# A norm's transposes move from the slot that projects values to the next slot, which projects outputs

## Chip, cores and metric

One Trainium2 chip, one of its cores. The metric is device microseconds (us) from the start to the end of one execution. The kernel before was run three times; the median is what the change is compared with. One further execution was recorded by the hardware profiler, and all durations of single instructions come from that one.

## What is computed

A transformer block in float32 for two sequences (B = 2) of 1024 rows with 256 features, and for each a context of 154 rows with 192 features. There are 16 heads of 64.

```python
h = layernorm(x, ln1);  x = attention(h, h, sa_wq, sa_wk, sa_wv, sa_wo) + sa_bo + x
h = layernorm(x, ln2);  x = attention(h, context, ca_wq, ca_wk, ca_wv, ca_wo) + ca_bo + x
h = layernorm(x, ln3);  p = h @ ff_w1 + ff_b1
out = (p[:, :1024] * gelu(p[:, 1024:])) @ ff_w2 + ff_b2 + x
# attention: softmax(q k^T / 8) v for each of 16 heads
```

## The kernel before

TensorE (PE) does all matmuls and transposes, VectorE (DVE) the maxima of the scores and the 32x32 block transposes of the weights, ScalarE (ACT) the exponentials and most copies out of PSUM, GpSimd (POOL) the scaling by the reciprocal sums and small arithmetic, and the queue of SyncE (SP) issues nearly all DMAs. Every engine works through its instructions in the order in which the program emits them (`manual_schedule`), so the Python order below is each engine's order.

**Self-attention** is a loop over 128 steps `p` (line 1062). A unit is one sequence and one pair of heads; there are 16 units (eight pairs of the first sequence, then eight of the second), and each has eight steps. Every step starts with `self_first`: two groups of scores (L488, 16 instructions each) into the two `ps_s` banks, and two maxima (L650). After that come, in this order: the stores left over from the step before (`flush(stores)`), the four exponentials (L499), the exchange of maxima and sums by four small DMAs (L509), POOL's joining of the step before (L517 to L525, with an ACT exponential at L521), two block transposes on DVE (L614), an addition to x if one is due (L469), and a reciprocal (L596) with four scalings on POOL (L600). The rest of the step is one of these, by p mod 8:

- 0 and 1: the next unit's queries, then keys (L357).
- 4, called the value slot here: the next unit's values (L388).
- 5, called the output slot: two pieces of the output projection (L462), and in some units an extra matmul group `context_ends` (L743).
- 2, 3, 6 and 7, called sum slots: half of a sum of values weighted by the transposed weights (L535) into two accumulators `po`. Slot 2 or 6 opens the two accumulators, 3 or 7 closes them; in the step after that ACT copies them out (L635).

What a slot's matmuls leave in PSUM is copied out by a "store" that is not emitted at once: it waits in the list `stores` until the next step's `flush(stores)`, which stands behind that step's scores and ahead of its exponentials.

**The norms beside it.** While these steps run, the norm that is needed next is done bit by bit. `norm_beside` puts steps k into the list `side`; `run_work` takes one of them in the value slot and one in the output slot of a unit, behind the value projection and ahead of the output pieces. Two norms are done so inside self-attention: the first norm of the second sequence (called at unit 1, so steps k = 0, 1, 2 ... fall on p = 12, 13, 20, 21, 28, 29 ...), and the second norm of the first sequence (called at unit 9, p = 76, 77, 84, 85 ...). For these two, which `narrow` tells from the other three, a step k handles one tile of 128 rows (n = 1); pairs of tiles are then worked on together:

- statistics (DVE, L235 and L236) at every k up to 7,
- the deviation of a pair (POOL, L241 and L245) at k = 2, 4, 6, 8, so always in a value slot,
- `normalize` of a pair (DVE L251, then two ACT instructions L265 into the tile `xn`, of which there is one buffer) at k = 3, 5, 7, 9, so always in an output slot,
- `turn` of a pair (four TensorE transposes L275 from `xn` into one PSUM bank `ph`; its store is four ACT instructions L290, which apply gain and shift and write `hT`) at k = 4, 6, 8, 10, so always in a value slot.

Within a step k the functions run in the order of the tuple in line 330: `turn` first, `normalize` last.

The PSUM bank for `ph` comes from the pool `ps_o`, because both slots call `run_work` with `sum_tile`. That pool has two banks in all, tag `po`. It also holds the two accumulators of the sum slots and the bank `pe` of `context_ends`:

```python
ps_o = ctx.enter_context(tc.tile_pool(name="ps_o", bufs=2, space=bass.MemoryType.PSUM))   # L67
run_work(2 if p < SA - SH else 1, h % 2 or h == 0, sum_tile)                               # L1086
halves[h, "po"] = [bank(f"po_{h}_{a2}") for a2 in range(2)]                                # L623
```

After the loop come 48 steps of cross-attention and then the feed-forward part, whose norms are not `narrow` and keep their steps.

Of the kernel before, what the change touches and what calls it, by code (L numbers as in the profile page):

```python
# [18 lines left out]
def tile_transformer_block(ctx: ExitStack, tc: tile.TileContext, a: dict, out: bass.AP):  # L19
# [12 lines left out]
    NT = S // P  # L32
# [64 lines left out]
    for n in names:  # L97
        k = n_of[n]
# [200 lines left out]
    def tile_order(kind):  # L299

        if kind == "ff":
            return list(range(NT))
        return [t for i in range(NT // 2) for t in (i, NT // 2 + i)]

    def narrow(kind, b):

        return kind == "sa" or kind == "ca" and b < B - 1

    def add_biases(kind, b):

        bo = {"sa": "sa_bo", "ca": "ca_bo", "ff": "ff_b2"}[kind]

        def add(t):
            xs = xt[b, t // GT][:, t % GT, :]
            nc.gpsimd.tensor_tensor(xs, xs, bias[bo], ALU.add)

        later.extend(lambda t=t: add(t) for t in range(NT))
        if b == B - 1 and kind != "ff":
            later.append(lambda: load_bias({"sa": "ca_bo", "ca": "ff_b2"}[kind]))

    def norm_beside(kind, b):

        after = {"sa": None, "ca": "sa", "ff": "ca"}[kind]
        stats, deviation, normalize, turn = norm_pieces(kind, b)
        n = 1 if narrow(kind, b) else 2
        lag = {}
        for fns, first in ((turn, 3), (stats, 0), (deviation, 1), (normalize, 2)):  # L330
            for i, fn in enumerate(fns):
                t = i if fns is stats else 2 * i + 1
                lag.setdefault(first + t // n, []).append((fn, fns is turn))
        for k in range(NT // n + 3):
            tiles = tile_order(kind)[k * n:(k + 1) * n]
            needs = [(after, b, half, t) for half in range(NQ) for t in tiles if after]

            def step(fns=lag[k]):
                done = [fn() for fn, _ in fns]
                return next((fn for fn in done if fn), None)  # L340

            side.append((any(turns for _, turns in lag[k]), needs, step))
        if not narrow(kind, b):
            side.append((False, (), lambda: add_biases(kind, b)))

# [198 lines left out]
    side, lates = [], []  # L544
# [118 lines left out]
    def self_beside(ui):  # L663

        nxt = self_pieces(*units[ui + 1]) if ui + 1 < NU else cross_pieces(*units[0])
        if ui + 1 < NU:
            work.extend(nxt)
        else:

            work.extend(nxt[:1])  # L670
            held.extend(nxt[1:])
        if ui >= HP:
            ob, og = divmod((ui - HP) // HP, NQ)
            t0 = (ui % HP) * 2
            out_pieces("sa", ob, og, out_order("sa")[t0:t0 + 2])
        if ui == 1:
            norm_beside("sa", 1)
        if ui in (4, 6):
            add_biases("sa", (ui - 4) // 2)
        if ui == NPAIR + 1:  # L680
            norm_beside("ca", 0)
# [214 lines left out]
    def cross_beside(ui):  # L896

        if ui == 2:
            norm_beside("ca", B - 1)
        if ui > HP + 1:  # L900
            ob, og = divmod((ui - HP - 2) // HP, NQ)
            t0 = ((ui - HP - 2) % HP) * 2
            out_pieces("ca", ob, og, out_order("ca")[t0:t0 + 2])
        if ui == NU - 5:
            norm_beside("ff", 0)
# [98 lines left out]
    with tc.manual_schedule():  # L1004
        stats, deviation, normalize, turn = norm_pieces("sa", 0, True)
# [56 lines left out]
        for p in range(SA):  # L1062
# [21 lines left out]
            if h == 0 or hg < LAG:  # L1084
# [4 lines left out]
                ui, n = divmod(p, 2 * SH)  # L1089
# [13 lines left out]
        for c in range(CA):  # L1103
# [13 lines left out]
            ui, n = divmod(c, len(CG))  # L1117
# [125 lines left out]
```

## Time and profile before

| | us |
|---|---|
| median of three runs | 1113.07 (1111.95 to 1114.58) |
| the profiled execution, whole | 1114.26 |
| its span, first to last instruction | 1112.5 |
| PE busy | 1092.5 |
| DVE, POOL, ACT busy | 855.3, 684.7, 626.1 |
| first scores of self-attention | at 17.63 |
| scores of its unit 15 (last) | at 673.2 |

A row of the timeline reads: start in us, duration in us of the merged instructions, engine, source line, operation, tile written <- tiles read, shape, number of instructions. Square brackets at the end give how long the engine stood idle just before and what ended that idle time. For matmuls the duration runs from the first start to a modelled end, so neighbours may overlap by some tenths of a microsecond. A row of the busy windows reads: stretch, its length, then busy time and number of instructions for PE, weight loads, DVE, ACT and POOL, the granted TensorE clock (1.00 is full), the share of DMA engines in use, and GB/s.

### The profile page before, as it was taken

Reading aid. Unit: us, or ns where it says so; the run is one execution under the profiler, and the core shown is the slowest. Engines: PE = TensorE matmul, PEld = TensorE weight load, DVE = VectorE, ACT = ScalarE, POOL = GpSimd, SP = SyncE. Lnnn points to the kernel's source line nnn. Section 1 sums busy time; section 2 is a strip of 40 time slices with the busy share of each in tenths; the row PEclk is TensorE's granted clock in tenths of the full one; section 3 lists DMA queues with packets and bytes.
Section 4 is the critical chain, followed back from the end, with each engine's and each line's share of the span. In section 5 each row is a group of like instructions: output and inputs, shape, how many; then the busy total and the mean of one; then the engine's idle time right before and its main releaser. Section 6 shows DMA issues by size and latency. Waiting matters only on the chain.

```text
span 1112.5 us, 44903 instructions
## 1 busy us (share of the span) xinstructions
PE 1092.5 (98%) x18452; PEld 732.9 (66%) x18452; DVE 855.3 (77%) x1205; ACT 626.1 (56%) x2025; POOL 684.7 (62%) x1584
## 2 busy tenths in 40 slices
PE   8999999999999999999999999999999999999998
PEld 6555666556757555566565565566766677888887
DVE  4889999898988989999999989978777885422212
ACT  4666666766666656666666766565556553121111
POOL 2777777777878777777777877776656653220000
PEclk9999999999999999999999999999999999999999
DMA  2222212121112011111111111046765553000000
GB/s 81 69 56 58 56 28 52 41 53 42 34 42 49 14 41 37 33 42 33 32 42 24 41 33 26 21 98 159 166 153 136 117 116 79 10 11 10 20 10 19
DMA packets 103983, 60.73 MB, mean 55 GB/s; under 512 B 32218, under 2 KB 94562, under 8 KB 103778
## 3 DMA queue, kind: packets, MB, share of 16 engines
q1 hardware_dynamic: 102546, 57.20, 21.8%
q8 instruction: 146, 2.39, 0.9%
q10 hardware_dynamic: 1232, 0.66, 0.2%
q14 instruction: 59, 0.48, 0.1%
HBM read 27.91 MB, written 2.10 MB: 27 GB/s over the span
## 4 chain that ended last, share of the span: by engine, by line
PE 63%; ACT 9%; DMA 7%; POOL 7%; DVE 7%; issue 3%; SPq 3%; DVEq 0%; POOLq 0%; ACTq 0%
PE pa L959 10%; PE po L535 10%; PE s L488 10%; ACT p L499 8%; DMA st<-st 6%; PE pf L982 5%; PE py_ca L462 5%; DVE st L650 4%; PE pq_ca L357 4%; PE poc L877 4%; SPq L509 3%; PE py_sa L462 3%; PE sc L798 3%; PE pv_sa L388 3%; PE pk_sa L357 3%
## 5 line engine op out<-in xcount | busy, mean ns | idle before, releaser
L499 ACT ACTIVATE p<-s,st 128x512 f32<-128x512 f32 x512 | 345.3, 687 | 195.4 <-DVE st L650 185.2
L600 POOL TENSOR_SCALAR p<-p,rd,ee 128x512 f32<-128x512 f32 x512 | 387.7, 772 | 46.8 <-DVE rd L596 45.9
L650 DVE TENSOR_REDUCE st<-s 128x2 f32<-128x1024 f32 x256 | 300.9, 1216 | 22.6 <-PE s L488 9.7
L614 DVE STREAM_TRANSPOSE pT<-p 128x1024 f32<-128x1024 f32 x256 | 302.3, 1218 | 0.3 <-POOL p L600 0.3
L488 PE MATMUL s<-k_sa,q_sa 64*32 64x512 f32 x4096 | 263.9, 593 | 8.6 <-ACT p L499 7.6
L535 PE MATMUL po<-pT,v_sa 64*32 64x256 f32 x8192 | 241.2, 376 | 1.7 <-DVE pT L614 1.4
L535 PEld LDWEIGHTS po<-pT,v_sa 64*32 64x32 f32 x8192 | 178.1, 106 | 71.9 <-issue 19.2
L488 PEld LDWEIGHTS s<-k_sa,q_sa 64*32 64x32 f32 x4096 | 82.6, 106 | 113.5 <-ACT p L499 61.9
L814 ACT ACTIVATE p<-sc,neg 128x154 f32<-128x154 f32 x256 | 96.4, 406 | 83.5 <-DVE rden L822 78.4
L825 POOL TENSOR_SCALAR p<-p,rden 128x154 f32<-128x154 f32 x256 | 97.3, 401 | 71.6 <-DVE rden L822 71.3
L968 DVE SCALAR_TENSOR_TENSOR u<-pa,cols,gate 128x256 f32<-128x256 f32 x64 | 30.9, 483 | 123.1 <-ACT gate L965 123.1
L959 PE MATMUL pa<-hT_ln,wf 128*128 128x256 f32 x512 | 121.1, 380 | 0.0
L965 ACT ACTIVATE gate<-pa,cols 128x256 f32<-128x256 f32 x64 | 30.4, 475 | 147.4 <-PE pa L959 144.1
L959 PEld LDWEIGHTS pa<-hT_ln,wf 128*128 128x128 f32 x512 | 96.7, 190 | 13.8 <-issue 0.9
L499 ACT ACTIVATION_READ_ACCUMULATOR p<-s,st 128x1 f32 x512 | 103.9, 203 | 0.0
L388 PEld LDWEIGHTS pv_sa<-sa_wv,hT_ln 64*128 64x128 f32 x1024 | 59.0, 188 | 14.6 <-issue 5.0
L982 PE MATMUL pf<-wf,u 128*128 128x256 f32 x256 | 64.7, 379 | 0.0
L523 POOL TENSOR_TENSOR zz<-ee,st 128x8 f32<-128x8 f32 x128 | 26.0, 203 | 60.4 <-ACT ee L521 60.4
L388 PE MATMUL pv_sa<-sa_wv,hT_ln 64*128 64x128 f32 x1024 | 62.2, 275 | 0.3 <-ACT v_sa L397 0.3
L462 PE MATMUL py_sa<-sa_wo,o_sa 128*128 128x256 f32 x256 | 59.7, 385 | 0.0
L462 PE MATMUL py_ca<-ca_wo,o_ca 128*128 128x256 f32 x256 | 59.7, 381 | 0.0
L357 PE MATMUL pk_sa<-hT_ln,sa_wk 64*32 64x512 f32 x960 | 58.2, 591 | 1.0 <-DMA st<-st 0.8
(89 smaller groups left out, 1253.6 us busy)
## 6 DMA issues: line engine op xcount, KB each, us to landing
wf<-pT_ca SPq DMA_DIRECT2D x128, 128.0 KB, 2.4
st<-st SPq DMA_DIRECT2D x512, 1.0 KB, 1.8
v_sa<-v_sa SPq DMA_DIRECT2D x32, 256.0 KB, 3.8
sa_wq<-in_L_xattn_sa_wq_dram SPq DMA_DIRECT2D x32, 128.0 KB, 3.0
sa_wk<-in_L_xattn_sa_wk_dram SPq DMA_DIRECT2D x32, 128.0 KB, 2.9
sa_wv<-in_L_xattn_sa_wv_dram SPq DMA_DIRECT2D x32, 128.0 KB, 3.3
ca_wq<-in_L_xattn_ca_wq_dram SPq DMA_DIRECT2D x32, 128.0 KB, 3.8
wf<-in_L_xattn_ff_w_dram SPq DMA_DIRECT2D x12, 256.0 KB
```

The lines of the kernel that those rows point to most:

```text
L357: nc.tensor.matmul(pq[r][f:f + m, at:at + n], lhsT=wt[own, c, f:f + m], rhs=h[own, c, t0:t0 + n], start=(c == 0), stop=(c == NH - 1), tile ...
L388: nc.tensor.matmul(pv[r][:, i * P:(i + 1) * P], lhsT=h[own, c, i * P:(i + 1) * P], rhs=wt[own, c, :], start=(c == 0), stop=(c == NH - 1), ...
L462: nc.tensor.matmul(py[:, e * D:(e + 1) * D], lhsT=o[:, i, (t + e) * P:(t + e + 1) * P], rhs=wo[kind][:, g * HP + i, :], start=(i == 0), st ...
L488: nc.tensor.matmul(sc[a4 * KB:(a4 + 1) * KB, j, :], lhsT=q[r, c:c + KB], rhs=k[r, h * HB:(h + 1) * HB], start=True, stop=True, tile_positi ...
L499: nc.scalar.activation(pr[:, j, :], sc[:, j, :], AF.Exp, bias=st[:, 0, 0, i, j:j + 1], accum_out=st[:, 0, 1, i, j:j + 1],)
L535: nc.tensor.matmul(po[a2][d:d + KB, :QH // 2], lhsT=v[r, t, e, d:d + KB], rhs=pT[r, d // DH * NK + n, :], start=(t == 0 and e == 0), stop= ...
L600: nc.gpsimd.tensor_scalar(pr[:, j, :], pr[:, j, :], rd[:, c:c + 1], ee[:, 0, c:c + 1], op0=ALU.mult, op1=ALU.mult,)
L614: nc.vector.transpose(halves[h][:, :, c:c + KB], groups.pop(0).rearrange("p j (n k) -> p (j n) k", k=KB))
L650: nc.vector.tensor_reduce(st[:, 0, 0, i, :], sc[i], AX.X, ALU.max, negate=True)
L825: nc.gpsimd.tensor_scalar(pr_[:, j, i, :T], pr_[:, j, i, :T], rden[:, j, i:i + 1], 1.0, op0=ALU.mult, op1=ALU.mult,)
L959: nc.tensor.matmul(pa[:, half, :TF * P], lhsT=w1[:, c, half * DF + f * P:half * DF + (f + 1) * P], rhs=h[:, c, t0 * P:(t0 + TF) * P], star ...
L982: nc.tensor.matmul(sums[blk][i][:, :D], lhsT=sums[blk, "u"][:, f, i * P:(i + 1) * P], rhs=w2[:, f, :], start=(f == 0), stop=(f == NF - 1),)
```

## The change

For the two `narrow` norms `turn` starts at k = last = 4 in place of 3, so it falls on k = 5, 7, 9, 11: output slots, p = 29, 37, 45, 53 and p = 93, 101, 109, 117 in place of p = 28, 36, 44, 52 and p = 92, 100, 108, 116. There is one step more per norm; k = 10 is then empty. The other norms keep last = 3.

```diff
@@ -327,19 +327,21 @@
         stats, deviation, normalize, turn = norm_pieces(kind, b)
         n = 1 if narrow(kind, b) else 2
         lag = {}
-        for fns, first in ((turn, 3), (stats, 0), (deviation, 1), (normalize, 2)):
+
+        last = 4 if narrow(kind, b) else 3
+        for fns, first in ((turn, last), (stats, 0), (deviation, 1), (normalize, 2)):
             for i, fn in enumerate(fns):
                 t = i if fns is stats else 2 * i + 1
                 lag.setdefault(first + t // n, []).append((fn, fns is turn))
-        for k in range(NT // n + 3):
+        for k in range(NT // n + last):
             tiles = tile_order(kind)[k * n:(k + 1) * n]
             needs = [(after, b, half, t) for half in range(NQ) for t in tiles if after]
 
-            def step(fns=lag[k]):
+            def step(fns=lag.get(k, ())):
                 done = [fn() for fn, _ in fns]
                 return next((fn for fn in done if fn), None)
 
-            side.append((any(turns for _, turns in lag[k]), needs, step))
+            side.append((any(turns for _, turns in lag.get(k, ())), needs, step))
```

## Prediction

> **What bounds the kernel now.** I read the page first: how busy each engine is, and the chain that ended last.
>
> ```profile
> PE 1092.5 (98%) x18452; PEld 732.9 (66%) x18452; DVE 855.3 (77%) x1205; ACT 626.1 (56%) x2025; POOL 684.7 (62%) x1584
> PE 63%; ACT 9%; DMA 7%; POOL 7%; DVE 7%; issue 3%; SPq 3%; DVEq 0%; POOLq 0%; ACTq 0%
> ```
>
> PE is busy almost without a break. So the question is not what the moved work costs, but whether PE, which takes its instructions in order, meets a new wait. From PE's timeline I took the start of the scores of all 128 steps; differences give the length of each step on PE. A sum slot takes 5.17 to 5.20 us in most units, an output slot 5.53 (6.10 or 6.32 with L743), a value slot 5.63 to 5.98 without the transposes and 6.21 to 6.72 with them. These are PE's own lengths nearly everywhere.
>
> Then the timeline around one place, steps 92 to 94:
>
> ```profile
> 526.65 0.66 PE L275 MATMUL ph_ln<-ident,xn_ln 128*128 128x128 f32 x4
> 527.24 1.95 PE L488 MATMUL s<-k_sa,q_sa 64*32 64x512 f32 x32
> 527.71 1.52 ACT L290 ACTIVATE hT_ln<-ph_ln,cols 128x128 f32<-128x128 f32 x4
> 529.11 3.72 PE L462 MATMUL py_sa<-sa_wo,o_sa 128*128 128x256 f32 x16
> 532.41 0.22 ACT L521 ACTIVATE ee<-dd 128x8 f32<-128x8 f32 x1
> 533.86 0.44 DVE L251 SCALAR_TENSOR_TENSOR off_ln<-mv_ln,rstd_ln 128x2 f32<-128x2 f32 x1
> 534.33 1.09 ACT L265 ACTIVATE xn_ln<-x,off_ln,rstd_ln 128x256 f32<-128x256 f32 x2 [1.70 <-DVE off_ln L251]
> 534.51 3.66 PE L535 MATMUL po<-pT,v_sa 64*32 64x256 f32 x128
> 535.46 0.69 ACT L499 ACTIVATE p<-s,st 128x512 f32<-128x512 f32 x1
> ```
>
> The reader is to see three things. The transposes (value slot, 526.65) have their store on ACT at 527.71 to 529.23, five us before the accumulators `po` of step 94 are opened (534.51). The next pair's normalize, in output slot 93, makes ACT wait 1.70 us for DVE's `off` and ends at 535.42. ACT's exponentials of step 94 follow at once.
>
> Last, one place where before already has what the change adds, step 46: `pe` was written in output slot 45, and its store stands behind the normalize on ACT.
>
> ```profile
> 271.87 1.09 ACT L265 ACTIVATE xn_ln<-x,off_ln,rstd_ln 128x256 f32<-128x256 f32 x2 [0.86 <-DVE off_ln L251]
> 272.86 0.30 ACT L748 COPY ends<-pe 128x192 f32<-128x192 f32 x1
> 272.26 0.63 PE L535 MATMUL po<-pT,v_sa 64*32 64x256 f32 x8
> 273.21 3.44 PE L535 MATMUL po<-pT,v_sa 64*32 64x256 f32 x116 [0.32 <-ACT ends L748]
> ```
>
> The first eight matmuls go into the bank that is free; the next need the bank that `pe` had, and PE stands until ACT has copied it.
>
> **The moved transposes: nothing.** Eight times four transposes (0.66 us on PE, no DMA, nothing on POOL or SP) leave the value slot and join the output slot that follows. In before both slots run at PE's own length, so their sum stays. `xn` has one buffer, and now the next normalize is emitted behind `turn` in the same step; but the transposes come right after the scores (near 529 in step 93) and normalize not before 534.33, so this wait is hidden by 5 us. The data are needed later still: the store of step 54 (about 315.6) against the first query projection at 327.1, that of step 118 (about 664.2) against step 120 at 673.2.
>
> **The moved store: a new wait for PE.** The store is emitted in the sum slot, behind the normalize of the output slot. ACT is in order, so the store can't start before normalize is through, and normalize waits for `off`, which DVE reaches only behind its reciprocal. That reciprocal hangs on POOL's and ACT's joining (L517 to L525), which does not get earlier: POOL runs without a break from its scalings at 527.52 to the joining at 532.31. Behind the waiting store stand the exponentials of the sum slot; behind the waiting `po` matmuls on PE stands everything. The last user of one of the two `po` banks is now `ph`, so after eight of 128 matmuls (0.23 of 3.66 us) PE waits until normalize start + 1.09 + 1.52:
>
> - step 30: 182.33 + 2.61 = 184.94, less 182.49 + 0.23: 2.22 us
> - step 38: 227.75 + 2.61 = 230.36, less 226.55 + 0.23: 3.58
> - step 46: 274.48, then `pe`'s copy 0.30: 274.78, against 273.21 in before: 1.6
> - step 94: 534.33 + 2.61 = 536.94, less 534.74: 2.20
> - step 102: 578.19 + 2.61 = 580.80, less 578.37: 2.43
> - step 110: 621.64 + 2.61 = 624.25, less 622.06: 2.19
> - steps 54 and 118 have no normalize ahead: the store follows L521 (ends 314.08 and 662.71) and is over at 315.6 (`pe`'s copy 315.9) and 664.23, before `po` at 316.74 and 664.58: nothing.
>
> Sum 14.2 us. **What is given back.** Where a later step is longer than PE's own length, because another engine or an exchange was late, a PE that comes later waits less. Up to the next place these surpluses are 0.8 us after step 30, 2.0 after 38, 0.4 after 46, 0.9 after 94, 0.95 after 102, none after 110. All given back would leave 14.2 - 5.05 = 9.2. But the others are late too: ACT by the store's 1.52, and what hangs on PE's scores by all of it. I take the middle, 12 us, and keep 9.2 and 14.2 as ends.
>
> **The clock.** New idle stretches of PE of 2.0 to 3.4 us may cost more than themselves. The longest in self-attention before:
>
> ```profile
> 699.56 0.66 PE L488 MATMUL s<-k_sa,q_sa 64*32 64x512 f32 x8 [1.68 <-ACT p L499]
> ...
> 700.00:702.00 2.00, 1.75 (x32) 0.18 (x16) 1.83 (x4) 1.56 (x7) 0.95 (x5) 0.84 0.00 0
> 702.00:704.00 2.00, 2.00 (x11) 1.17 (x4) 2.00 (x3) 0.62 (x2) 2.00 (x3) 0.50 0.04 2
> 704.00:706.00 2.00, 2.00 (x14) 1.01 (x21) 2.00 (x3) 2.00 (x8) 1.42 (x5) 0.81 0.01 0
> ```
>
> After 1.68 us idle (and 0.25 more a microsecond later) the granted clock fell to 0.84, 0.50 and 0.81 in three stretches of 2 us: 2 x (0.16 + 0.50 + 0.19) = 1.7 us of PE time lost. After idles of 1.58 (before 34.40) and 1.42 us (before 729.01) it stayed at 1.00. So a drop depends on more than the length; all six new idles are longer than the one that brought it. Ends: no drop, 0, and six, 10.2 us. I take three, 5.1 us, as three such idles in before brought one drop and the new ones are longer.
>
> The Trainium skill ("TensorE: Matmul & The Clock Gate", section "HAM oscillation — how this bites in real kernels") has PE throttled by idle gaps over about 3.4 us. By that rule only step 38 would come near, and the sum would have one drop at most (1.7 us in place of 5.1); the drop after 1.68 us above speaks against so high a limit, and the rows decide.
>
> **Sum.** 12 + 5.1 = 17.1 us on the profiled execution's 1114.26 gives 1131.4; that execution lies 1.2 us above the median, so the median becomes 1113.07 + 17.1 = 1130.2. About 0.2% (2.2 us) is what a measurement of this kernel can tell from no change.
>
> **Rivals.**
>
> A. Stalls without a clock drop: 1113.07 + 9.2 to 14.2, so 1122 to 1127, middle 1125. For: two idles near 1.5 us left the clock alone. It is the forecast's lower part.
>
> B. The bank wait does not arise (the accumulators get a bank other than `ph`'s, or PE reaches it late), and only the exponentials of six sum slots come 1.52 us later. In step 94 they would end at 539.56, where the second group of scores of step 95 wanted its bank near 538.9: 0.6 us at least, 1.5 at most, six times: 4 to 9 us, middle 1119.5. Against: step 46 shows the wait.
>
> C. Faster. ACT no longer has 1.52 us of store ahead of the output slot's exponentials, and scores of that slot start 0.6 us earlier (DVE's maximum waited 0.55 us for them in step 93). If through this normalize came 2.2 us earlier, store and `po` would not meet, and the surplus of the eight value slots over 6.21 (0.28, 0.51, 0.21, 0.37, 0.22, 0.51, 0.21, 0) would go: 2.3 us, 1110.8. It decides at a normalize start of 532.1 in place of 534.33. Against: `off` follows a reciprocal that POOL sets, and POOL does not move.
>
> D. The cost is given back entirely, since ACT is idle 44% of the time: 1113, within 0.2%. Against: PE's total surplus between the places is 5 us, the stalls 14.
>
> **How the numbers follow.** Forecast with at least one drop 0.60; A 0.20; B 0.10; C 0.05; D 0.05. Forecast and A go from 1113.07 + 9.2 = 1122.3 to 1113.07 + 14.2 + 10.2 = 1137.5. The range reaches down into B: 1118 to 1137. Faster 0.05, same 0.05, slower 0.90.
>
> **What would show it.** Right: L290's last eight groups stand right behind L265 or L521 in sum slots; a group of L535 with idle time put down to ACT `hT_ln` L290, six times, 2.0 to 3.4 us each; steps 30, 38, 46, 94, 102 and 110 longer by 1.6 to 3.6 us, 54 and 118 not; clock below 1.00 in the two or three stretches after some of them. Value slots 0.6 us shorter, output slots 0.6 longer. Wrong: no idle at L535 with that releaser (B or C), normalize in step 93 starting near 532 (C), or stalls that the next unit takes back (D).

## The result and the profile after

Four runs of the changed kernel have a median of 1128.25 us (1126.13 to 1131.93), four of the kernel before 1112.51: ratio 1.0149, 95% interval 1.0131 to 1.0166. It is slower by 15.7 us. The profiled execution took 1129.17 us, 14.9 more than that of before; its span is 1127.4. Two lines came in below `norm_beside`, so what was L488, L499, L521, L535 and L748 is L490, L501, L523, L537 and L750 here.

The page after: busy engines, the chain that ended last, and the group of the weighted sums with its idle time ahead; last, the same group in the page of before.

```profile
PE 1095.6 (97%) x18452; PEld 745.8 (66%) x18452; DVE 855.2 (76%) x1205; ACT 626.7 (56%) x2025; POOL 682.1 (61%) x1584
PE 56%; ACT 11%; POOL 8%; DMA 8%; DVE 8%; issue 4%; SPq 4%; DVEq 0%; POOLq 0%; ACTq 0%
L537 PE MATMUL po<-pT,v_sa 64*32 64x256 f32 x8192 | 251.5, 384 | 15.6 <-ACT hT_ln L290 14.2
L535 PE MATMUL po<-pT,v_sa 64*32 64x256 f32 x8192 | 241.2, 376 | 1.7 <-DVE pT L614 1.4
```

The number of matmuls is the same and the busy times hardly change. New is the last column of the third line: 14.2 us in which PE stood in front of these matmuls until ACT had finished `hT_ln`, the moved store. In before that column held 1.7 us, and no ACT store of `hT_ln` in it.

The timeline of the changed kernel around step 94, all engines (the same place as shown of before):

```profile
533.22 0.65 PE L275 MATMUL ph_ln<-ident,xn_ln 128*128 128x128 f32 x4
537.26 0.21 ACT L523 ACTIVATE ee<-dd 128x8 f32<-128x8 f32 x1 [0.24 <-POOL dd L521]
538.69 0.44 DVE L251 SCALAR_TENSOR_TENSOR off_ln<-mv_ln,rstd_ln 128x2 f32<-128x2 f32 x1
539.00 0.63 PE L537 MATMUL po<-pT,v_sa 64*32 64x256 f32 x8
539.23 1.10 ACT L265 ACTIVATE xn_ln<-x,off_ln,rstd_ln 128x256 f32<-128x256 f32 x2 [1.75 <-DVE off_ln L251]
540.23 1.48 ACT L290 ACTIVATE hT_ln<-ph_ln,cols 128x128 f32<-128x128 f32 x4
541.60 0.69 ACT L501 ACTIVATE p<-s,st 128x512 f32<-128x512 f32 x1
541.76 5.09 PE L537 MATMUL po<-pT,v_sa 64*32 64x256 f32 x116 [2.14 <-ACT hT_ln L290]
```

The transposes were done at 533.87. ACT was free at 537.47, but the next thing in its order was the normalize, which waited 1.75 us for DVE; the store came behind it. PE did eight matmuls into the free bank and stood for 2.14 us. The same idle in PE's timeline at the other five places (steps 30, 38, 46, 102 and 110):

```profile
185.25 3.44 PE L537 MATMUL po<-pT,v_sa 64*32 64x256 f32 x116 [2.13 <-ACT hT_ln L290]
232.81 3.44 PE L537 MATMUL po<-pT,v_sa 64*32 64x256 f32 x116 [3.31 <-ACT hT_ln L290]
279.01 5.37 PE L537 MATMUL po<-pT,v_sa 64*32 64x256 f32 x128 [2.13 <-ACT hT_ln L290]
589.51 5.11 PE L537 MATMUL po<-pT,v_sa 64*32 64x256 f32 x116 [2.54 <-ACT hT_ln L290]
636.55 5.13 PE L537 MATMUL po<-pT,v_sa 64*32 64x256 f32 x116 [1.96 <-ACT hT_ln L290]
```

The 116 matmuls behind the idle take 3.44 us in steps 30 and 38, and 5.1 in 94, 102 and 110: there the clock fell. In step 46 the idle stands ahead of all 128 matmuls, because both banks of the pool were lent out there, one to `ph` and one to `pe`. The busy windows around step 94, then around step 38, where PE stood longest:

```profile
540.00:542.00 2.00, 0.24 (x8) 0.23 (x16) 2.00 (x3) 2.00 (x6) 1.91 (x5) 0.93 0.01 1
542.00:544.00 2.00, 2.00 (x48) 0.98 (x40) 2.00 (x3) 2.00 (x7) 0.04 (x1) 0.50 0.01 4
...
230.00:232.00 2.00, 0.00 (x0) 0.00 (x0) 2.00 (x3) 1.73 (x5) 2.00 (x4) 1.00 0.23 67
232.00:234.00 2.00, 1.19 (x48) 0.92 (x56) 2.00 (x3) 2.00 (x8) 0.99 (x4) 1.00 0.01 4
```

**Where the 14.9 us are.** Starts of the scores give the length of every step on PE. Against the profiled execution of before, in us:

| | change |
|---|---|
| sum slots 30, 38, 46, 94, 102, 110 | +2.38, +3.19, +3.41, +4.02, +4.46, +3.90 = +21.4 |
| of this idle at L537 before hT_ln | 2.13, 3.31, 2.13, 2.14, 2.54, 1.96 = 14.2 |
| of this four clock drops (46, 94, 102, 110) and rest | 7.2 |
| sum slots 54 and 118 | 0.0 |
| eight value slots | -4.65 |
| eight output slots | +3.27 |
| all other steps of self-attention | -4.5 |
| after self-attention | -0.6 |

### The profile page after: what moved, and what is told of

Read it like the earlier page. It is cut to its first block, busy times and chain, and to the rows that moved or that the text cites. A ratio compares the mean times of both kernels' runs of the same rounds, so it can differ in the third digit from the quotient of the medians.

```text
span 1127.4 us, 44911 instructions
## 1 busy us (share of the span) xinstructions
PE 1095.6 (97%) x18452; PEld 745.8 (66%) x18452; DVE 855.2 (76%) x1205; ACT 626.7 (56%) x2025; POOL 682.1 (61%) x1584
## 3 DMA queue, kind: packets, MB, share of 16 engines
q1 hardware_dynamic: 102546, 57.20, 21.4%
## 4 chain that ended last, share of the span: by engine, by line
PE 56%; ACT 11%; POOL 8%; DMA 8%; DVE 8%; issue 4%; SPq 4%; DVEq 0%; POOLq 0%; ACTq 0%
PE pa L961 10%; PE po L537 10%; ACT p L501 9%; PE s L490 8%; DMA st<-st 6%; DVE st L652 5%; PE pf L984 5%; PE py_ca L464 5%; PE pq_ca L359 4%; PE poc L879 4%; POOL p L602 4%; SPq L511 4%; PE sc L800 3%; PE py_sa L464 2%; PE pk_sa L359 2%
## 5 line engine op out<-in xcount | busy, mean ns | idle before, releaser
L501 ACT ACTIVATE p<-s,st 128x512 f32<-128x512 f32 x512 | 346.0, 688 | 214.1 <-DVE st L652 200.1
L490 PE MATMUL s<-k_sa,q_sa 64*32 64x512 f32 x4096 | 266.6, 595 | 8.1 <-ACT p L501 7.2
L537 PE MATMUL po<-pT,v_sa 64*32 64x256 f32 x8192 | 251.5, 384 | 15.6 <-ACT hT_ln L290 14.2
L537 PEld LDWEIGHTS po<-pT,v_sa 64*32 64x32 f32 x8192 | 185.2, 108 | 88.1 <-issue 21.8
L490 PEld LDWEIGHTS s<-k_sa,q_sa 64*32 64x32 f32 x4096 | 90.4, 106 | 105.4 <-ACT p L501 53.9
L501 ACT ACTIVATION_READ_ACCUMULATOR p<-s,st 128x1 f32 x512 | 104.8, 205 | 0.0
L598 DVE RECIPROCAL rd<-den 128x4 f32<-128x4 f32 x128 | 22.4, 175 | 49.7 <-POOL den L527 44.1
L359 PE MATMUL pq_sa<-hT_ln,sa_wq 64*32 64x512 f32 (+1 forms) x976 | 59.0, 586 | 0.0
```

The lines of the kernel that those rows point to most:

```text
L359: nc.tensor.matmul(pq[r][f:f + m, at:at + n], lhsT=wt[own, c, f:f + m], rhs=h[own, c, t0:t0 + n], start=(c == 0), stop=(c == NH - 1), tile ...
L490: nc.tensor.matmul(sc[a4 * KB:(a4 + 1) * KB, j, :], lhsT=q[r, c:c + KB], rhs=k[r, h * HB:(h + 1) * HB], start=True, stop=True, tile_positi ...
L501: nc.scalar.activation(pr[:, j, :], sc[:, j, :], AF.Exp, bias=st[:, 0, 0, i, j:j + 1], accum_out=st[:, 0, 1, i, j:j + 1],)
L537: nc.tensor.matmul(po[a2][d:d + KB, :QH // 2], lhsT=v[r, t, e, d:d + KB], rhs=pT[r, d // DH * NK + n, :], start=(t == 0 and e == 0), stop= ...
```

## The experiments

Theory: the moved store waits on ACT behind a normalize that waits for DVE; PE waits for its bank; some of the waits lower the clock. Ratios are to the kernel before on the same chip.

**1. The store ahead of the normalize (e1_store_first).** Transposes in the output slot as in the changed kernel, store emitted at once:

```diff
-                done = [fn() for fn, _ in fns]
+                done = []
+                for fn, turns in fns:
+                    made = fn()
+                    if turns and narrow(kind, b):
+                        made = made()
+                    done.append(made)
```

> As the changed kernel, the transposes in the output slot, but their store is emitted in the same step, ahead of the normalize. Theory (PE waits for a PSUM bank whose store stands on ACT behind the normalize, which waits for DVE): the store runs right after L523, near 2 us ahead of the accumulators; the six idles at L537 put down to L290 (14.2 us in the changed kernel) and the four clock drops go, and what remains is the difference of the two slots (value slots 4.65 us shorter, output slots 3.27 longer in the changed kernel): before minus 1.4 us, so ratio 0.997 to 1.000. Rival (the transposes themselves cost in the output slot, or whatever holds the bank there): it stays at 1.010 or above.

Measured: 1113.22 us, ratio 1.0009 (0.9992 to 1.0026). Its timeline around step 94:

```profile
533.25 1.49 ACT L290 ACTIVATE hT_ln<-ph_ln,cols 128x128 f32<-128x128 f32 x4
534.59 3.65 PE L542 MATMUL po<-pT,v_sa 64*32 64x256 f32 x124
535.04 1.09 ACT L265 ACTIVATE xn_ln<-x,off_ln,rstd_ln 128x256 f32<-128x256 f32 x2 [0.30 <-DVE off_ln L251]
```

The store now fills the time in which ACT waited for `off`, and no idle of PE is put down to it here. Of the six idles two short ones are left, 0.47 us at step 38 and 0.45 us at step 46. No loss can be told from the scatter any more, with the transposes still in the output slot. The 1.4 us that the slots should have brought are not seen: its value slots were 4.8 us shorter and its output slots 3.5 longer, but other steps took that back, and the interval leaves out 0.9987.

**2. The store held, the transposes not moved (e2_store_held).**

```diff
-        for fns, first in ((turn, last), (stats, 0), ...
+        for fns, first in ((turn, 3), (stats, 0), ...
...
+                held_one = kept_back.pop() if kept_back else None
+                if made:
+                    kept_back.append(made)
+                return held_one
```

> The transposes back in the value slot as in the kernel before, and only their store is held one step longer, so that it stands behind the normalize in the sum slot. Theory: the same six idles at L537 put down to L290, about 2.0 to 3.4 us each, 14 us together, and clock drops after three or four of them: ratio 1.012 to 1.018, though no transpose is moved. Rival (the place of the transposes on PE costs): ratio 1.000.

Measured: 1129.88 us, ratio 1.0158 (1.0134 to 1.0181). Two of its six idles in PE's timeline, at steps 38 and 94 (the others are 2.08, 2.12, 1.93 and 1.80 us):

```profile
230.69 5.13 PE L543 MATMUL po<-pT,v_sa 64*32 64x256 f32 x116 [3.03 <-ACT hT_ln L290]
545.54 5.02 PE L543 MATMUL po<-pT,v_sa 64*32 64x256 f32 x116 [3.11 <-ACT hT_ln L290]
```

The loss is there without a transpose moved; five clock drops follow the idles, one more than expected. With the first experiment this shows that the place of the store is what costs, and the place of the transposes is not.

**3. PE kept at work during the wait (e3_filler).**

```diff
+        if part == 0:
+            for i in range({6: 16, 8: 24, 22: 16, 24: 16, 26: 16}.get(h, 0)):
+                nc.tensor.transpose(po[0][:, 2 * P + i % 2 * P:][:, :P], ident, ident)
         for t in range(NT // 2 * part, NT // 2 * (part + 1)):
```

> As the changed kernel, but ahead of the accumulating matmuls of steps 30, 38, 94, 102 and 110 PE does 16 (step 38: 24) transposes of the identity into the unused half of the free accumulator's bank, about 0.13 us each, 2 to 3 us in the time in which it otherwise waits; step 46 has no free bank and gets none. Theory (four clock drops of 1.7 us on top of the idles): the drops after steps 94, 102 and 110 go, that after step 46 stays; the steps 94, 102, 110 last 7.4 to 7.7 us in place of 9.1 to 9.7, and the time falls by 5 to 6 us against the changed kernel: ratio near 1.009. Rival (the added length of these three steps is not the clock's): no change, 1.015; if the filler is itself on the path, slower than that.

Measured: 1124.42 us, ratio 1.0102 (1.0083 to 1.0120), some 5 us less than the changed kernel's 1.0149, and the intervals do not meet. In its profile the only stretch of self-attention below full clock is at step 46, 278 to 282 us. Steps 94, 102 and 110 last 8.28, 7.25 and 7.25 us in place of 9.22, 9.65 and 9.10. Steps 30 and 38, filled as well but without a drop in the changed kernel, are not shorter (7.89 and 8.76 us; in the changed kernel 7.58 and 8.76). The idle left in step 94:

```profile
543.85 3.44 PE L537 MATMUL po<-pT,v_sa 64*32 64x256 f32 x116 [0.79 <-ACT hT_ln L290]
```

So about a third of the loss is the clock, and it goes when PE has something to do.

**4. Normalize on POOL (e4_normalize_pool).** The store stays in the sum slot. The branch under the changed line is POOL's, the other one ACT's.

```diff
-                if not narrow(kind, b) or first and i == 1:
+                if not first or i == 1:
```

> As the changed kernel, store in the sum slot, but the normalize of the second half of the work (L265, ACT) is done by POOL (L262, 0.55 us each in place of 0.60). Theory: the store has nothing to wait for on ACT and runs right after L523, no idle at L537 is put down to L290, no clock drop; POOL gets 8 x 1.1 us more on a chain that sets some steps: ratio 0.995 to 1.003. Rival (it is the sum slot that makes the store late, with or without the normalize ahead of it): 1.010 to 1.015.

Measured: 1114.06 us, ratio 1.0009 (0.9995 to 1.0022). Around step 94:

```profile
530.80 1.49 ACT L290 ACTIVATE hT_ln<-ph_ln,cols 128x128 f32<-128x128 f32 x4
532.29 3.70 PE L537 MATMUL po<-pT,v_sa 64*32 64x256 f32 x128
534.79 1.10 POOL L262 TENSOR_SCALAR xn_ln<-x,rstd_ln,off_ln 128x256 f32<-128x256 f32 x2
```

The store is emitted in the sum slot as in the changed kernel, yet it runs at 530.80, since nothing that waits stands ahead of it. Of the six idles one of 0.5 us is left (step 38). The sum slot as such is not too late; the waiting instruction ahead of the store is.

**5 and 6. One norm at a time (e5_first_norm_only, e8_second_norm_only).**

```diff
-        last = 4 if narrow(kind, b) else 3
+        last = 4 if kind == "sa" else 3                       # e5
+        last = 4 if kind == "ca" and narrow(kind, b) else 3   # e8
```

> Only the first norm of the second sequence gets the later turn (steps 29, 37, 45, 53); the second norm of the first sequence keeps steps 92, 100, 108, 116. Theory (each place costs its own idle and, in some executions, a clock drop): three idles at L537 put down to L290 after steps 30, 38 and 46 (2.1, 3.3, 2.1 us), none at 94, 102, 110; 6 to 10 us, ratio 1.005 to 1.009. Rival (the cost is not local, the whole loop falls behind once the order is changed): 1.013 or more, or units 11 to 14 longer too.

> Only the second norm of the first sequence gets the later turn (steps 93, 101, 109, 117). Theory: idles at L537 put down to L290 after steps 94, 102 and 110 alone, about 2.1, 2.5 and 2.0 us, 6 to 12 us with clock drops, ratio 1.006 to 1.011; together with the other half's time the changed kernel's 15.7 us within 3 us. Rival (not local): 1.013 or more.

Measured: 1.0070 (1.0044 to 1.0096) and 1.0066 (1.0041 to 1.0090). The idles lie at 30, 38, 46 alone (2.38, 3.33, 2.26 us) and at 94, 102, 110 alone (2.25, 2.16, 1.94). Together 13.6 thousandths against 14.9: the cost is local and adds up, within the intervals. How many drops a half had differs: one in e5's self-attention sum slots, two in e8's.

**7. The exponentials late, no bank (e6_act_delay).** From the kernel before; four ACT instructions write a scratch tile where the changed kernel has its store.

```diff
+    def idle_work():
+        for _ in range(4):
+            nc.scalar.activation(scratch, ident, AF.Identity, bias=cols[:, 0:1], scale=cols[:, 1:2])
...
+                if narrow(kind, b) and k in (5, 7, 9):
+                    return idle_work
```

> The kernel before, with four more ACT instructions of 128x128 from SBUF into a scratch tile behind each normalize of steps 29, 37, 45, 93, 101, 109, emitted where the changed kernel has its store; no PSUM bank hangs on them. It puts the rival price on the exponentials' delay of 1.5 us alone. Rival B of the prediction: 4 to 9 us, ratio 1.004 to 1.008. Theory: PE has work of its own in a sum slot until about the time at which the late exponentials end, so most of the 1.5 us is hidden: below 4 us, ratio 1.000 to 1.004, no idle of PE above 1 us in these steps.

Measured: 1.0107 (1.0084 to 1.0129), more than both sides said. Its timeline, first around step 94, then at step 46:

```profile
543.34 2.06 ACT L325 ACTIVATE scratch<-ident,cols 128x128 f32<-128x128 f32 x4
545.30 0.67 ACT L507 ACTIVATE p<-s,st 128x512 f32<-128x512 f32 x1
546.78 1.09 PE L496 MATMUL s<-k_sa,q_sa 64*32 64x512 f32 x16 [0.74 <-ACT p L507]
...
279.02 5.13 PE L543 MATMUL po<-pT,v_sa 64*32 64x256 f32 x116 [2.50 <-ACT ends L756]
```

Two things make it larger than meant: the four instructions take 2.06 us, not 1.52, and at step 46 a bank does hang on them after all, since the store of `pe` stands behind them (2.50 us of idle). There and at step 38 the clock dropped. Steps 30, 94, 102 and 110, clean of both, lose 1.54, 1.45, 2.01 and 1.89 us over two steps each. So PE has no work of its own to cover late exponentials: the expectation that most of the delay is hidden was wrong. Late exponentials alone would cost much of what the bank costs. In the changed kernel the two waits seem to overlap: there the steps that follow (31, 95, 103, 111) are not longer, here each of them is, by 0.5 us. That is read from the lengths of the steps; no run separates the two.

**8. The bank late, the exponentials on time (e9_store_after_exp).** The counterpart: the changed kernel with the store behind the exponentials of the sum slot. `kept` is a list that the program already has; each step empties it behind its exponentials and scalings.

```diff
+                made = next((fn for fn in done if fn), None)
+                if made and narrow(kind, b):
+                    kept.append(made)
+                    return None
+                return made
```

> As the changed kernel, but the moved store is emitted one place later in the sum slot, behind that step's four exponentials and L523, so the exponentials have no store ahead of them and only the bank comes late. It is the counterpart of the kernel that delayed the exponentials without a bank. Theory (PE waits for the bank): the store ends near 2.6 us plus 0.3 us later than in the changed kernel, the idles at L537 put down to L290 become about 4.5 to 5.5 us at steps 30, 38, 46, 94, 102 and 110, and 54 and 118 get one of 1 to 3 us as well; every idle is so long that a stretch of 3.41 us holds 1.8 us of it, so a clock drop follows each of the six: 28 us of idle and 10 us of clock, ratio 1.025 to 1.040. Rival (the cost is the late exponentials, which are on time here): ratio below that of the changed kernel, 1.000 to 1.010.

Measured: 1170.76 us, ratio 1.0487 (1.0458 to 1.0517). Two of its idles, in steps 94 and 118:

```profile
568.04 6.28 PE L541 MATMUL po<-pT,v_sa 64*32 64x256 f32 x116 [5.56 <-ACT hT_ln L290]
721.46 6.37 PE L541 MATMUL po<-pT,v_sa 64*32 64x256 f32 x116 [4.47 <-ACT hT_ln L290]
```

All eight places now have a long idle (40.0 us in all) and a clock drop behind it, 6.8 us long at seven of them; 54 and 118 cost as much as the others, and most drops last twice as long as expected, so the ratio lies above the expected range. The rival falls: the exponentials of step 94 begin at 563.71, right behind the normalize, and with them on time and the bank later the loss is 55.5 us in place of 15.7.

**9. The changed kernel again, for the clock (e7_again).**

> The changed kernel once more, for the clock. In the first profile drops began at about 278.92, 541.72, 589.52, 637.32 and 715.8 us, whose distances are multiples of 3.413 us, and each lasted 3.4 us. Theory (the clock is set on a fixed grid of 3.41 us by how long PE stood still in the stretch just ended): again all drops begin on one grid, shifted against the first; an idle brings a drop where 1.8 us or more of it lies in one stretch of the grid, and none where a boundary cuts it so that neither part has that. Rival (length alone decides): the idle of 3.3 us at step 38, the longest, brings a drop first.

Measured: one execution of 1135.39 us (the kernel before on the same chip: 1116.15), with drops from about 186.6, 548.4, 596.2, 644.0 and 722.5 us. Two of its idles (steps 30 and 38):

```profile
186.54 5.13 PE L537 MATMUL po<-pT,v_sa 64*32 64x256 f32 x116 [2.35 <-ACT hT_ln L290]
235.97 3.44 PE L537 MATMUL po<-pT,v_sa 64*32 64x256 f32 x116 [3.29 <-ACT hT_ln L290]
```

The idle of 2.35 us was followed by a drop and that of 3.29 us was not, so length alone does not decide. The expected limit of 1.8 us failed once: at step 46 an idle of 2.22 us had 1.86 us in one stretch of the grid, and no drop came. More on this below. The drops differ from execution to execution (here at 30, 94, 102, 110; before that at 46, 94, 102, 110), which is part of the scatter of this kernel.

**10. A filler for a gap that the kernel before has (e10_fill_gap).** An attempt at a version better than both.

```diff
+                if p == SA - SH:
+                    fill = sum_tile("fill")
+                    for i in range(12):
+                        nc.tensor.transpose(fill[:, i % 4 * P:][:, :P], ident, ident)
```

> The kernel before, with twelve transposes of the identity, 1.6 us, into a free bank of ps_o in step 124, where PE stood idle for 1.68 us before the scores of step 125 and the clock then dropped for 3.4 us. Seen in eight of the ten profiles so far. Theory (PE standing still lowers the clock): no drop near 700 us, up to 1.7 us less in the executions that had it: ratio 0.998 to 1.000, at the limit of what can be measured; the profile shows no clock below 0.99 there. Rival (filling is on the path): ratio above 1.001.

Measured: 1113.64 us, ratio 0.9985 (0.9966 to 1.0004). The windows where the clock was 0.84 and 0.50 before:

```profile
700.00:702.00 2.00, 1.76 (x33) 0.36 (x18) 1.84 (x4) 1.47 (x6) 0.94 (x5) 1.00 0.00 0
702.00:704.00 2.00, 2.00 (x8) 1.27 (x8) 2.00 (x3) 0.72 (x3) 2.00 (x4) 1.00 0.04 2
```

No drop in its profile, and the filler's effect on the clock shows in the other executions too: the mean granted clock was 1.000 in ten of its twelve, and in five of the seventeen of the kernel before. A gain in time is not shown: the interval holds 1.

## Why the prediction was right

The forecast was 1130.2 us, 17.1 more; measured 1128.25, 15.7 more. By its steps:

- **The wait for the bank**: right in place and cause, and in size place by place within 0.3 us but for step 46. Six idles were named, 14.2 us summed, none at 54 and 118; the profile has those six, 14.2 us together, none at 54 and 118. That the sums agree to a tenth is luck: step 38 was 3.31 us in place of 3.58, step 46 2.13 in place of 1.6. For step 46 the prediction let PE do eight matmuls first, as in before; with both banks lent out it stands ahead of the first, and from 272.26 the prediction's own reckoning gives 2.2 us. The order of ACT's queue was enough, because the row of step 46 in before had shown the same wait with another tile.
- **The moved transposes, priced at nothing**: nearly. Value slots became 0.58 us shorter each, output slots 0.41 longer: -1.4 us. Experiment 1 did not turn this into time.
- **Given back, 2.2 us taken**: 5.1 by the table (4.5 in self-attention, 0.6 after it), of which 1.8 can be tied to the waits. Steps 39 and 40 are together 1.08 us shorter than in before in the changed kernel and in every other profile with the idle at step 38, but not in the four without it (e1, e4, e8, e10); steps 104 and 105 are 0.74 shorter in the same way, with the idle at 102 (0.55 in e9). The rest lies in places like steps 71, 72 and 74, where e1 and e4, which have no wait, show the same 0.4 to 0.7 us each: there the profiled execution of before was long by chance. So the term was about right, and the comparison of two single executions adds some 3 us of scatter.
- **The clock, three drops at 1.7 us, 5.1 us**: four drops of 3.41 us at half clock, 6.8 us in the profile. The filler took away three of them and 5 us, which agrees. The reason given for the number ("the new ones are longer") was not the right one: the longest idle, step 38, had no drop. How many come depends on where the grid lies (four here, four in e7, five in e2), so a count of three was near by luck.
- **The sum** was 17.1 against 14.9 in the profiles: the clock was 1.7 us too low, the two slots 1.4 us too high, what came back 2.9 us too low (only 1.8 of the 5.1 can be tied to the waits), and 0.4 us is the rest of the sum slots. These errors cancel in part, so the close total says less than the six idles do.
- **Rival A** (no drops, 9.2 to 14.2 us): three of the filler's five executions had a mean clock of 1.000, and they lost 9.7, 11.3 and 12.8 us, so it was the right price of the case without drops. **Rival B** (late exponentials alone, 4 to 9 us): the bank decides, as experiment 8 shows, but B's 0.6 to 1.5 us a place was too low a price for a delay of that kind; 1.45 to 2.0 us were measured for a delay of 2.06. **Rival C** needed a normalize near 532.1 in step 93; it did not come earlier: it began 1.97 us after the scores of step 94 (539.23, 537.26), in before 1.57 us after them (534.33, 532.76). **Rival D** had 5 us of surplus against 14 of idle, and so it came.

## What to carry to other kernels

On an engine that works in order, ask what an instruction will stand behind, not only what it costs: the same copies, 1.5 us in each of eight places, cost nothing that could be measured ahead of an instruction that waits, and 15.7 us of the whole behind it. A PSUM bank that is lent out for a side task must be back before its next owner comes, so the copy that frees it belongs ahead of anything on that engine that waits for a third engine. When PE is the bound, its waits can cost half as much again through the clock (here 6.8 us on 14.2).

## What the runs showed of the hardware

The granted clock falls on a fixed grid, that is, only at the ends of equal stretches of 3.413 us. In the changed kernel's first profile the drops begin at about 278.92, 541.72, 589.52, 637.32 and 715.8 us (the last, in step 124, is the one that before has near 701); the distances are 77.0, 14.0, 14.0 and 23.0 times 3.413 us. In experiment 9 they are 106.0, 14.0, 14.0 and 23.0 times that, from another start; each of these drops to half the clock lasted about 3.4 us, and after the seven idles of 4.5 to 6.2 us in experiment 8 it lasted 6.8, two stretches. In the sum slots from step 30 on, in all profiles, a drop began where 1.93 us or more of an idle lay in one stretch of the grid, and none began at 1.79 or less; between these both happened. So the 3.31 us of step 38 cost no clock: a boundary at 231.13 cut it into 1.63 and 1.68. In e5, whose grid lay otherwise, an idle of 3.33 us at the same step had 2.85 us in one stretch, and the clock fell. This limit is not a general one: in step 124 of e5 1.63 us was enough, and in experiment 8 a drop went on after a stretch with only 0.85 us of idle (step 118). What else counts is not shown.

The Trainium skill ("TensorE: Matmul & The Clock Gate", section "What's actually happening") describes a free-running window of 3413 ns; the distances above agree. The rule that PE is throttled by gaps over about 3.4 us ("HAM oscillation — how this bites in real kernels") does not hold here: idles of 1.96 to 2.54 us brought the drop, and in the sum slots what separated those with a drop from those without was how much of one window was idle.
